# A four-layer graph network on one core: layer 3's graph loaded by transfers, a fourth attention tile, narrower projection matmuls, values spread through DRAM, and all jobs listed in a new order

## The chip, the core and the metric

The kernel runs on one core of a Trainium2 chip. Its engines are TensorE (PE, with its weight loads shown as PEld), VectorE (DVE), ScalarE (ACT), GpSimd (POOL) and SyncE (SP), which here only issues DMAs. Each engine works through its own list of instructions in order and waits on semaphores where it needs another's result. The metric is device time in microseconds, the median of several executions. All durations below are from one profiled execution.

## What is computed

There are 32 batches of 512 nodes with 64 features, and one 512 x 512 weighted graph `adj`, for the most part zero. Four layers follow one another; each normalises its input (layernorm, then maximum with 0), applies a graph network, and adds the result to its input:

```python
# layer 0: three steps, W1 and W2 are linear maps, v's node 0 is set to a given value
effects = adj @ v ; v = relu([v, effects] @ W1.T + b1) @ W2.T + b2
# layer 1: twice
z = relu((adj @ z) @ weights[i])
# layer 2: 8 heads with 64 -> 128 features, then one output attention of 64 features
h = x @ W ; s = (h @ h.T) * graph ; s = where(s == 0, -1e16, s)
out = softmax(s) @ h + b                 # leaky_relu(0.01) behind the heads, and behind the output
# layer 3: the graph's diagonal is set to 1
h = x @ w3 ; e = adj * leaky_relu(h @ a_src + (h @ a_dst).T, 0.2)
out = softmax(e) @ h + bias
```

## The kernel before

**Tiles.** Two batches make a pair; there are 16 pairs. Feature-by-node tiles hold two batches of 64 features on 128 partitions and 512 nodes in the free dimension. An attention tile `sm` is 128 x 8 x 512 (512 x 512 weights of one head, for two batches or two heads at a time by column groups); there are three such buffers, in the pool `ap`. PSUM is split into four buffers `s` for scores (`ps_s`) and four `mm` for all else (`ps_m`). A weighted sum takes all four `mm` buffers from its first part to its eviction.

**Stages of a pair.** `front` computes layers 0 and 1 in 25 steps F0 to F24: transposes (L327), per-node products (`by_nodes`, L347), aggregation over nodes (`aggregated`, L335, and L381), layernorms. Then come:

- eight units `Heads`, four for each batch of the pair: scores (`gram`, L445, with the mask added as a matmul at L448), row maxima with the graph as factor (L466, on DVE), their negation (L473, POOL), exponentials with row sums (L477, ACT), normalisation (reciprocal L487 on DVE, products L489 on POOL), transposition in blocks of 32 (L495, DVE). Units are taken two by two for the weighted sum (`weigh`, L505), its eviction `us` (L560), the head's matrix (L539), leaky ReLU into `y` (L550), and the projection (L568), whose result is collected in `cat` (L581, L584). The keys `Y` come from `ZZ` and the heads' Gram matrices (L827, L837).
- one unit `Out`: layer 2's output attention over `HH`. `features` (L589, L591) makes HH from cat by a matmul with II, which sums the two halves of the partitions and leaves the sum in both; `nodes` (L612, L598) transposes HH to node rows `hn`.
- the chain oA to oN: layernorm of x3, transposition to zT3, `weights` (L670, L672) for h3T, `nodes` (L681) for the rows h3n and the source terms `src` (L690, moved by four small DMAs, L695).
- one unit `Last`: layer 3. Its target row times ones (`pd`, L720) stays in one of the four `s` buffers; ACT's Prelu writes scores into sm (L722), and maxima are taken from there with the graph `A3` as factor, a second copy of adj in SBUF with ones on its diagonal (`loops`).

`Ends` (L779) sums the values of `Out` of one pair and `Last` of the pair before it together; its eviction is L798 and L800, its residuals L808 and L814. Inputs for keys are transposed twice for each pair (`features_of`, L419, once for each batch, z being laid out in two copies, L295). Values for the weighted sums must lie in groups of 32 partitions, four times over: `quarters` makes them by 16 DMAs of 32 KB each from tile to tile (L310), but for the last pair or two by a write to DRAM and four loads of 128 KB (L320, L304).

**Order.** Nothing is scheduled by the compiler: the order in which Python issues is the order on each engine. Each job (one score group, one maximum, one part of a sum) has a name and a place: `PLACES` gives a tick offset and a rank inside the tick, ten ticks make a round, and one round works on one pair's heads, on Out of the pair before, on Last of the pair before that, and on later pairs' fronts. `TAIL` lists the jobs behind the last regular tick; a short table places the jobs of the start. SP's DMAs are part of the jobs, so they stand in the same order, and a DMA that waits holds those behind it.

Of the kernel before, what the change touches and what calls it, by code (L numbers as in the profile page):

```python
# [21 lines left out]
def gnn_stack_kernel(  # L22
# [19 lines left out]

# [11 lines left out]

    def blk(t):
        return slice(t * P, (t + 1) * P)
# [7 lines left out]
    ap_ = ctx.enter_context(tc.tile_pool(name="ap", bufs=3))  # L80
# [6 lines left out]
    def mm_ps():  # L87

        return ps_m.tile([P, N], F32, tag="mm", name="mm")


# [12 lines left out]
    A3 = const.tile([P, NS, N], F32, name="A3")  # L104
    A2 = const.tile([P, NS, N], F32, name="A2")
    ident = const.tile([P, P], F32, name="ident")
# [3 lines left out]
    early1 = hp.tile([P, 4, P], F32, tag="h3T", bufs=1, name="early1")  # L110
# [3 lines left out]
    w3a = const.tile([P, P + 2], F32, name="w3a")  # L114
    w3bd = w3a[:, 0:P]
    a1bd = const.tile([P, 2], F32, name="a1bd")
    a2bd = const.tile([P, 2], F32, name="a2bd")
# [11 lines left out]
    for z0, value in ((mhalf, -0.5), (ones, 1.0), (NP, 0.0), (w3a, 0.0), (a1bd, 0.0), (a2bd, 0.0)):  # L129
        nc.gpsimd.memset(z0, value)  # L130
# [22 lines left out]
    for j, r in enumerate(R):  # L153
        nc.sync.dma_start(out=w3bd[r, r], in_=w3)
        nc.sync.dma_start(out=a1bd[r, j : j + 1], in_=a3[0:D, :])
        nc.sync.dma_start(out=a2bd[r, j : j + 1], in_=a3[D : 2 * D, :])
# [3 lines left out]


# [9 lines left out]
    II = const.tile([P, 2, D], F32, name="II")  # L171
    II2 = II.rearrange("p k d -> p (k d)")
    NEGM = const.tile([P, NT, N], BF16, name="NEGM")
    a2rep = const.tile([P, P], F32, name="a2rep")
# [11 lines left out]
    def graph_turned():  # L186
        for s in range(NT):
            pt = mm_ps()
            for t in range(NT):
                nc.tensor.transpose(pt[:, blk(t)], A[:, t, blk(s)], ident)  # L190
            (nc.scalar.copy, nc.vector.tensor_copy)[s % 2](AT[:, s, :], pt)
# [20 lines left out]
    def masks():  # L212

        for k in range(2):
            nc.vector.tensor_tensor(II[:, k, :], ident[:, 0:D], ident[:, D:P], ALU.add)

        nc.vector.tensor_scalar(NEGM, A, 0.0, NEG_INF, ALU.is_equal, ALU.mult)

    def loops():

        for s in range(NS):
            for base in (0, -D):
                nc.gpsimd.affine_select(
                    out=A3[:, s, hblk(s)],
                    in_=A3[:, s, hblk(s)],
                    pattern=[[-1, D]],
                    compare_op=ALU.not_equal,
                    fill=1.0,
                    base=base,
                    channel_multiplier=1,  # L230
                )
# [4 lines left out]

    def grams():

# [11 lines left out]
    def vectors():  # L250
        for j in range(2):
            nc.vector.tensor_scalar(a2rep[:, R[j]], ones[:, R[j]], a2bd[:, j : j + 1], None, ALU.mult)

        pt = mm_ps()
        nc.tensor.transpose(pt[:, 0:P], w3bd, ident)
        w3T = hp.tile([P, P], F32, tag="us", bufs=1, name="w3T")
        nc.vector.tensor_copy(w3T, pt[:, 0:P])
        pt = mm_ps()
        nc.tensor.matmul(pt[:, 0:2], lhsT=w3T, rhs=a1bd, start=True, stop=True)
        nc.vector.tensor_copy(w3a[:, P:], pt[:, 0:2])  # L260


    def ln_relu(xt, tag, bufs=2, copies=1):


# [18 lines left out]
        z = lp.tile([P, NT, 2, copies, D], F32, tag=tag, bufs=bufs, name="z")  # L284
        zf = z.rearrange("p t j c d -> p (t j) c d")
        nc.vector.scalar_tensor_tensor(  # L286
            zf[:, :, 0, :],
# [6 lines left out]
        if copies > 1:  # L294
            nc.gpsimd.tensor_copy(zf[:, :, 1, :], zf[:, :, 0, :])  # L295
        return z if copies > 1 else z[:, :, :, 0, :]

    def quarters(v, tag, rows=None):


        vq = hp.tile([P, N // 32, D], F32, tag=tag, bufs=1, name="vq")
        if rows is not None:
            for i in range(4):
                nc.sync.dma_start(  # L304
                    out=vq[32 * i : 32 * i + 32], in_=rows.rearrange("(jb r) d -> r jb d", r=32)
                )
            return vq
        for i in range(4):
            for k in range(4):
                nc.sync.dma_start(  # L310
                    out=vq[32 * i : 32 * i + 32].rearrange("r (t k) d -> r t k d", k=4)[:, :, k, :],
                    in_=v[32 * k : 32 * k + 32],
                )
        return vq

    def rows_of(v):

        rows = dr.tile([N, *v.shape[2:]], F32, tag=f"rows{len(v.shape)}", name="rows")
# [4 lines left out]
    def transposed(z, tag, bufs=2):  # L323

        pt = mm_ps()
        for t in range(NT):
            nc.tensor.transpose(pt[:, blk(t)], z[:, t].rearrange("p j d -> p (j d)"), ident)  # L327
        zT = lp.tile([P, N], F32, tag=tag, bufs=bufs, name="zT")
        nc.scalar.copy(zT, pt)
        return zT  # L330

    def aggregated(v, pe, first=True):

# [10 lines left out]

# [5 lines left out]
    def front(p, state):  # L350

# [10 lines left out]
        hT = transposed(v, "hT0")  # L362
        yield
        for step in range(STEPS):

# [16 lines left out]
            aggregated(v, ph, first=False)  # L382
            hT = lp.tile([P, N], F32, tag="hT0", name="hT0")
            nc.scalar.activation(hT, ph, AF.Relu, bias=b1k[k])
            yield
        pv = by_nodes(hT, W2T)
        x1 = xp.tile([P, NT, 2, D], F32, tag="x1", bufs=1, name="x1")
# [6 lines left out]
        for i in range(LAYERS):  # L394
            pe = mm_ps()
            aggregated(z, pe)
# [680 lines left out]
```

## Time and profile before

Three executions took 2306.47, 2307.35 and 2311.79 us; the median is 2307.35.

| | us | share of the span |
|---|---|---|
| profiled execution's own time, by its span | 2307.4 | |
| PE busy (matmuls) | 2186.1 | 95% |
| PEld busy (weight loads) | 1170.5 | 51% |
| DVE busy | 1858.7 | 81% |
| ACT busy | 1494.0 | 65% |
| POOL busy | 1299.3 | 56% |
| chain that ended last: PE / ACT / DVE / POOL | | 77% / 9% / 7% / 4% |
| DMA: 279,975 packets, 70.98 MB | | q1 (SP's): 17.1% of 16 engines |

A group's row reads: source line, engine, operation, output and input tiles, tile of the array, shape, count, then busy time, mean nanoseconds of one record, and the engine's idle time before the group with what ended it. An fp32 matmul shows as two records, so counts of such rows are twice those in the program. Rows in order of time begin with start and duration in microseconds. A row of a stretch has its bounds, its length, the busy times of PE, PEld, DVE, ACT and POOL with counts, the granted TensorE clock, and DMA.

The page's largest rows beside those shown in the prediction: exponentials (L477) 910.9 us on ACT, normalisation (L489) 871.3 on POOL, block transposes (L495) 769.8 and maxima (L466) 734.4 on DVE, scores (L445) 576.7 and weighted sums (L505) 500.9 on PE.

### The profile page before, as it was taken

To read this page: it belongs to the slowest core of one execution; us is meant where nothing else is said; L and a number is where in the kernel's file an instruction comes from. 1 tells how busy PE (TensorE), PEld (TensorE's weight loads), DVE (VectorE), ACT (ScalarE), POOL (GpSimd) and SP (SyncE) were. 2 spreads that over 40 slices of the span, in tenths; PEclk is the share of its full clock that TensorE was granted. 3 is DMA by queue.
4 is the path that set the end of the run, shared out by engine and by line. 5 is a ranking of instruction groups with operands and counts; after the bars stand their busy time and mean duration, and the time that the engine had idled before them with its cause. 6 is when DMAs were issued, how large, how long until landed. Compare 5 with 4: busy or idle time off the path is not lost.

```text
span 2307.4 us, 78438 instructions
## 1 busy us (share of the span) xinstructions
PE 2186.1 (95%) x32683; PEld 1170.5 (51%) x32683; DVE 1858.7 (81%) x4099; ACT 1494.0 (65%) x3754; POOL 1299.3 (56%) x2175
## 2 busy tenths in 40 slices
PE   7889999999999999999999999999999999998885
PEld 4335555555555555555554555555455555554443
DVE  3658788889888888988888898888889888888674
ACT  1446557667676666767666676766667676666564
POOL 2345465656656565665656566565656666565344
PEclk9899999999999999999999999999999999999987
DMA  5001111202121121212112121211212121021113
GB/s 123 11 15 21 25 21 23 42 15 39 20 41 27 21 42 17 38 21 39 29 19 42 19 39 20 36 32 18 41 21 36 23 31 32 15 37 23 29 29 57
DMA packets 279975, 70.98 MB, mean 31 GB/s; under 512 B 275004, under 2 KB 277060, under 8 KB 279620
## 3 DMA queue, kind: packets, MB, share of 16 engines
q1 hardware_dynamic: 278848, 65.80, 17.1%
q8 instruction: 256, 4.19, 0.8%
q14 instruction: 99, 0.81, 0.1%
q10 hardware_dynamic: 772, 0.17, 0.0%
HBM read 13.64 MB, written 4.98 MB: 8 GB/s over the span
## 4 chain that ended last, share of the span: by engine, by line
PE 77%; ACT 9%; DVE 7%; POOL 4%; issue 2%; DMA 1%; SPq 0%; ACTq 0%; POOLq 0%; DVEq 0%
PE s L445 21%; PE mm L505 16%; PE mm L335 10%; ACT sm L477 6%; PE mm L568 5%; PE mm L779 5%; PE mm L539 5%; PE s L448 5%; DVE sm L495 4%; PE mm L347 3%; PE mm L827 3%; DVE sm L466 2%; PE mm L381 2%; PE mm L612 1%; PE mm L589 1%
## 5 line engine op out<-in xcount | busy, mean ns | idle before, releaser
L477 ACT ACTIVATE sm<-sm,nmx 128x512 f32<-128x512 f32 x1280 | 910.9, 720 | 235.8 <-POOL nmx L473 235.4
L489 POOL TENSOR_SCALAR sm<-sm,rs 128x512 f32<-128x512 f32 x1280 | 871.3, 699 | 144.2 <-DVE rs L487 104.3
L466 DVE CUSTOM_DVE_ANT_0 sm<-s,A 128x512 f32<-128x512 f32 x1152 | 734.4, 679 | 138.3 <-PE s L448 113.5
L495 DVE STREAM_TRANSPOSE sm<-sm 128x1024 f32<-128x1024 f32 x640 | 769.8, 1224 | 38.6 <-POOL sm L489 37.7
L445 PE MATMUL s<-ZZ,Y 64*64 64x512 f32 x4096 | 576.7, 607 | 28.1 <-ACT Y L837 14.7
L505 PE MATMUL mm<-sm,vq 32*64 32x256 f32 (+1 forms) x17152 | 500.9, 378 | 24.5 <-DVE sm L495 11.4
L473 POOL TENSOR_SCALAR nmx<-mx 128x2 f32<-128x2 f32 x640 | 147.6, 234 | 582.1 <-DVE mx L466 526.8
L505 PEld LDWEIGHTS mm<-sm,vq 32*64 32x64 f32 x17152 | 399.2, 134 | 141.6 <-issue 62.1
L445 PEld LDWEIGHTS s<-ZZ,Y 64*64 64x64 f32 x4096 | 147.8, 133 | 256.8 <-issue 111.2
L448 PE MATMUL s<-NEGM,I2b 64*64 64x512 bf16 x2304 | 259.5, 378 | 0.0
L477 ACT ACTIVATION_READ_ACCUMULATOR sm<-sm,nmx 128x1 f32 x1280 | 250.7, 196 | 0.0
L560 ACT COPY us<-mm 128x256 f32<-128x256 f32 x256 | 76.2, 382 | 155.3 <-PE mm L505 155.0
L335 PE MATMUL mm<-AT,v 128*128 128x512 f32 x384 | 173.8, 595 | 0.0
L550 ACT ACTIVATE y<-mm,cols 128x512 f32<-128x512 f32 x256 | 159.2, 684 | 11.4 <-PE mm L539 11.3
L448 PEld LDWEIGHTS <-I2b 64*64 64x64 bf16 x2304 | 81.5, 107 | 160.5 <-issue 160.0
L273 POOL TENSOR_TENSOR xc<-x,nmu 128x512 f32<-128x512 f32 x48 | 54.8, 1141 | 182.9 <-DVE nmu L271 182.9
L539 PE MATMUL mm<-us,Wh 64*64 64x512 f32 x1024 | 134.0, 592 | 23.1 <-ACT us L560 23.1
L282 POOL TENSOR_TENSOR r<-ve,mhalf 128x8 f32<-128x8 f32 x64 | 110.8, 1731 | 45.2 <-DVE ve L280 41.4
L568 PE MATMUL mm<-y,Wo_sb 128*64 128x512 f32 x512 | 127.1, 605 | 0.0
L779 PE MATMUL mm<-sm,vq 32*64 32x256 f32 x3712 | 118.7, 381 | 4.0 <-DVE sm L495 2.6
L335 PEld LDWEIGHTS mm<-AT,v 128*128 128x128 f32 x384 | 73.5, 192 | 93.3 <-issue 92.5
L286 DVE SCALAR_TENSOR_TENSOR z<-xc,r 128x512 f32<-128x512 f32 x64 | 45.4, 709 | 93.2 <-POOL r L282 90.0
(135 smaller groups left out, 2073.6 us busy)
## 6 DMA issues: line engine op xcount, KB each, us to landing
vq<-z SPq DMA_DIRECT2D x512, 32.0 KB, 1.9
vq<-hn SPq DMA_DIRECT2D x480, 32.0 KB, 1.9
vq<-h3n SPq DMA_DIRECT2D x448, 32.0 KB, 1.9
A<-in_adj_dram SPq DMA_DIRECT2D x5, 1024.0 KB, 7.4
xt<-in_x_dram SPq DMA_DIRECT2D x32, 128.0 KB, 2.4
out_dram<-xo SPq DMA_DIRECT2D x32, 128.0 KB, 2.0
vq<-rows SPq DMA_DIRECT2D x24, 128.0 KB, 3.1
src<-src SPq DMA_DIRECT2D x64, 1.0 KB, 1.9
```

The lines of the kernel that those rows point to most:

```text
L335: nc.tensor.matmul(pe, lhsT=v[:, m].rearrange("p j d -> p (j d)"), rhs=AT[:, m, :], start=(first and m == 0), stop=(m == NT - 1),)
L445: nc.tensor.matmul(pss[half][R[ab], :], lhsT=lhsT, rhs=rhs, start=True, stop=False)
L448: nc.tensor.matmul(pss[half][R[ab], :], lhsT=I2b[R[half], :], rhs=NEGM[R[half], k, :], start=False, stop=True,)
L466: nc.vector.tensor_tensor_reduce(self.sm[:, s, :], src, graph, 1.0, -FMAX, ALU.mult, ALU.max, self.mx[:, s : s + 1])
L477: nc.scalar.activation(self.sm[:, s, :], self.sm[:, s, :], AF.Exp, bias=self.nmx[:, s : s + 1], accum_out=self.ssum[:, s : s + 1],)
L489: nc.gpsimd.tensor_scalar(self.sm[:, s, :], self.sm[:, s, :], self.rs[:, s : s + 1], 1.0, ALU.mult, ALU.mult)
L495: nc.vector.transpose(out=two, in_=two)
L505: nc.tensor.matmul(self.u[i][R[c], 0 : weights.shape[1] * 32], lhsT=values[32 * i : 32 * i + 32, jb, :], rhs=weights[32 * i : 32 * i + 32, ...
L539: nc.tensor.matmul(py[c][r, :], lhsT=Wh2[R[c], 2 * (self.q - 1 + c) + ab, r], rhs=self.us[R[c], 2 * ab : 2 * ab + 2].rearrange("p i (s e) ...
L550: nc.scalar.activation(y, py[c], AF.Prelu, bias=cols[:, h : h + 1], alpha=0.01)
L568: nc.tensor.matmul(pa[R[ab], :], lhsT=Wo_sb[:, h, :], rhs=self.y[h], start=(k == 0), stop=(k == 1),)
L779: nc.tensor.matmul(self.u[i][r, 0 : N // 2], lhsT=values[i // 2][q, jb, :], rhs=sm[q, :, 32 * jb : 32 * jb + 32], start=(jb == 0), stop=(j ...
```

## The change

- **Layer 3's graph.** A3 is no longer in SBUF. It is written once to DRAM (a copy of adj, with ones set on its diagonal by two DMAs), and for each pair `graphs` loads it in four slices of 512 KB into that pair's own attention tile (jobs g0e to g3e). `scores` of Last writes each block of 512 columns into an `s` buffer of PSUM, and the maxima read score and graph from there and from the tile.
- **Fourth attention tile.** The pool `ap` has four buffers.
- **Layer 3's target row.** w3a has two more columns, so that `nodes` yields source and target terms in one product. `values` (job oV) sends the target column to DRAM (`dst`), and `targets` (job de) loads it back into `pd`, spread over 64 partitions for each batch. The product h3T and the pd matmul are gone; the last pair makes pd by one matmul with w3d.
- **Projection by node halves.** `project` issues eight matmuls of 256 columns in place of four of 512. Partition half 0 of `cat` holds nodes 0 to 255, half 1 the others. HH is made from cat by four DMAs (job f), and hn by two transposes in place of four (jobs h and H).
- **Inputs transposed once.** z is no longer doubled. One set of four transposes gives ZZ for both batches; a second tile with the halves exchanged is filled by two DMAs (jobs zT and zE).
- **Values by way of DRAM**, in all pairs: rows are written once (`rows_of`), and four loads of 128 KB make each set of quarters.
- **Order.** Jobs are cut finer (evictions apart from the matmuls, negations apart from maxima; front has 33 steps), and three lists, HEAD, ROUND and TAIL, give all of them in one sequence. In ROUND a name carries the number of pairs by which it lags the round.

```diff
-    ap_ = ctx.enter_context(tc.tile_pool(name="ap", bufs=3))
+    ap_ = ctx.enter_context(tc.tile_pool(name="ap", bufs=4))
...
-    A3 = const.tile([P, NS, N], F32, name="A3")
+    A3 = dr.tile([P, NS, N], F32, tag="A3", bufs=1, name="A3")
...
-            nc.gpsimd.tensor_copy(zf[:, :, 1, :], zf[:, :, 0, :])
...
+    def quarters(rows, tag):
+        vq = hp.tile([P, N // 32, D], F32, tag=tag, bufs=1, name="vq")
+        for i in range(4):
+            nc.sync.dma_start(out=vq[32 * i : 32 * i + 32], in_=rows.rearrange("(jb r) d -> r jb d", r=32))
+        return vq
...
+    def features_of(p):
+        s = state[p]
+        pt = transposed(s["z"])
+        yield
+        s["ZZ"] = [lp.tile([P, N], F32, tag=f"ZZ{n}", name="ZZ") for n in range(2)]
+        nc.scalar.copy(s["ZZ"][0], pt)
+        for j in range(2):
+            nc.sync.dma_start(out=s["ZZ"][1][R[1 - j]], in_=s["ZZ"][0][R[j]])
+        yield
...
-                for k in range(2):
-                    for ab in range(2):
-                        h = 2 * (self.q - 1 + k) + ab
-                        nc.tensor.matmul(
-                            pa[R[ab], :],
-                            lhsT=Wo_sb[:, h, :],
-                            rhs=self.y[h],
+            order = [(k, ab) for ab in range(2) for k in range(2)]
+            for n, (k, ab) in enumerate(order):
+                for half in range(2):
+                    nc.tensor.matmul(
+                        self.pa[R[half], 0 : N // 2],
+                        lhsT=Wo_sb[:, self.head(k, ab), :],
+                        rhs=self.y[self.head(k, ab)][:, half * N // 2 : (half + 1) * N // 2],
...
-                nc.tensor.matmul(ph, lhsT=II2, rhs=self.cat, start=True, stop=True)
-                HH = hp.tile([P, N], F32, tag=f"HH{self.j}", bufs=1, name="HH")
-                nc.scalar.copy(HH, ph)
+            s["HH"][self.j] = hp.tile([P, N], F32, tag=f"HH{self.j}", bufs=1, name="HH")
+            for half in range(2):
+                for r in R:
+                    nc.sync.dma_start(
+                        out=s["HH"][self.j][r, half * N // 2 : (half + 1) * N // 2], in_=s["cat", self.j][R[half], :]
+                    )
...
-                nc.tensor.matmul(ph, lhsT=w3bd, rhs=s["zT3"], start=True, stop=True)
-                s["h3T"] = hp.tile([P, N], F32, tag="h3T", bufs=1, name="h3T")
-                nc.scalar.copy(s["h3T"], ph)
...
+            if self.p < NPAIR - 1:
+                s["dst"] = dr.tile([2, N], F32, tag="dst", name="dst")
+                for j in range(2):
+                    nc.sync.dma_start(out=s["dst"][j].rearrange("(t q) -> q t", q=P), in_=src[:, :, 2 + j])
+            self.rows3 = rows_of(h3n, "h3rows")
...
+        def graphs(self, k):
+            two = slice(2 * k, 2 * k + 2)
+            nc.sync.dma_start(out=self.sm[:, two, :], in_=A3[:, two, :])
+        def targets(self):
+            s = state[self.p]
+            if self.p == NPAIR - 1:
+                self.pd = score_ps()
+                nc.tensor.matmul(self.pd, lhsT=w3d, rhs=s["zT3"], start=True, stop=True)
+            else:
+                self.pd = hp.tile([P, N], F32, tag="pd", bufs=1, name="pd")
+                for j, r in enumerate(R):
+                    nc.sync.dma_start(out=self.pd[r], in_=s["dst"][j].partition_broadcast(D))
+        def scores(self, i):
+            self.pss[i] = score_ps()
+            nc.scalar.activation(
+                self.pss[i], self.pd, AF.Prelu, bias=state[self.p]["src"][:, i : i + 1], alpha=0.2
+            )
```

Two stretches of the new ROUND that the prediction speaks of, as they stand:

```
vD0:0 s0d:0 r7c:0 g2e:2 m2c:0 s1d:0 m3c:0 x2c:0 nAc:0 x3c:0 oN:2 nBc:0 s3d:0 us0:0 t1c:0 s2d:0 w00:0
oV:2 de:2 r2d:0 m1d:0 t3c:0 r7d:0 r6d:0 x1d:0 y00:0 m3d:0 s1f:1 nAd:0 r4d:0 r5d:0 k2:0
F15:-1 y10:0 o0:0 x3d:0 t0c:0 m2d:0 r3f:1 x2d:0 r2f:1 s3e:2
```

(s: a score group; r: a maximum; m: a negation; x: two exponentials; n: normalisation of half a tile; t: a block transpose; v: a quarter of a weighted sum; w, y, o, c: head matrix, leaky ReLU, projection, collecting; k, Y: keys. The last letter names the unit: a to d and g to j heads, f Out, e Last.)

## The prediction

> **What bounds the kernel now.** I read the page's table of busy times first, then the row of granted clock, then stretches of the span, then TensorE's instructions in order of time, then who waited for whom.
>
> ```profile
> span 2307.4 us, 78438 instructions
> PE 2186.1 (95%) x32683; PEld 1170.5 (51%) x32683; DVE 1858.7 (81%) x4099; ACT 1494.0 (65%) x3754; POOL 1299.3 (56%) x2175
> PEclk9899999999999999999999999999999999999987
> ```
>
> TensorE is busy 95% of the span, at full clock but for the two ends. Here a rule of the Trainium skill speaks against the plain reading: "Perfetto Trace Analysis", section "Identifying the Most-Contended Engine", holds that matmul busy time is no good measure of how near TensorE is to its limit, and wants the share of weight loads instead, which is only 51%. So I check by starts. One round of the loop (one pair of batches) in the steady middle:
>
> ```profile
> 1159.68 1.04 PE L539 MATMUL mm<-us,Wh 64*64 64x512 f32 x8
> 1160.54 1.04 PE L445 MATMUL s<-ZZ,Y 64*64 64x512 f32 x8
> 1161.40 0.40 PE L448 MATMUL s<-NEGM,I2b 64*64 64x512 bf16 x4
> 1161.61 1.04 PE L539 MATMUL mm<-us,Wh 64*64 64x512 f32 x8
> 1162.47 1.04 PE L827 MATMUL mm<-ZZ,G 64*64 64x256 f32 x16
> 1163.34 1.04 PE L445 MATMUL s<-ZZ,Y 64*64 64x512 f32 x8
> ```
>
> Start to start, a 512-column group takes 0.86 us although its record says 1.04: records overlap. L827, with half the columns and twice the instructions, takes 0.87: time follows columns streamed. The same L779 sum starts at 1094.88 and 1230.15, so a round is 135.3 us. Adding starts over that round (36 score groups at 1.07, five weighted sums at 7.1, five aggregations at 3.5, the rest about 37) gives 128.6 us of streaming. So TensorE really is the bound. Costs below are start to start. By the rule there would be half the engine to spare and nothing removed from TensorE would show; by the rows nearly all of it does.
>
> ```profile
> 203.10:1827.60 1624.50, 1595.28 (x24068) 853.03 (x24065) 1376.60 (x3038) 1106.59 (x2784) 960.62 (x1596) 1.00 0.17 29
> 2222.00:2307.40 85.40, 50.68 (x1138) 35.33 (x1136) 49.16 (x102) 43.50 (x109) 37.64 (x55) 0.79 0.34 57
> ```
>
> These are length, then busy time of PE, weight loads, DVE, ACT, POOL, then clock. In twelve rounds PE stands 29.2 us (2.4 a round); DVE is next at 85%. In the last 85 us nothing bounds but a chain of dependent steps, at clock 0.79.
>
> **What leaves TensorE.** The rows by form, and the same groups in order of time:
>
> ```profile
> L568 PE MATMUL mm<-y,Wo_sb 128*64 128x512 f32 x512 | 127.1, 605 | 0.0
> L589 PE MATMUL mm<-cat,II 128*128 128x512 f32 x64 | 33.0, 597 | 1.2 <-DVE cat L584 1.1
> L419 PE MATMUL mm<-ident,z 128*128 128x128 f32 x128 | 21.0, 287 | 1.8 <-POOL z L295 1.8
> L612 PE MATMUL mm<-ident,HH 128*128 128x128 f32 x128 | 20.0, 280 | 0.2 <-ACT HH L591 0.2
> L670 PE MATMUL mm<-zT,w3a 128*128 128x512 f32 x32 | 19.0, 676 | 2.0 <-ACT zT L329 2.0
> L720 PE MATMUL pd<-h3T,a2rep 128*128 128x512 f32 x32 | 17.2, 621 | 0.0
> ```
>
> ```profile
> 1193.34 1.13 PE L670 MATMUL mm<-zT,w3a 128*128 128x512 f32 x2
> 1194.31 1.06 PE L681 MATMUL mm<-w3a,zT 128*128 128x130 f32 x8
> ```
>
> Per round, from start to next start: L589 twice (0.96 and 0.86) is gone, cat now reaching HH by four transfers: 1.82. L670, whose product served only L720, goes: 0.97. L720 goes in 15 of 16 pairs, its row coming back by DRAM: 0.94. L419 is done once in place of twice: 0.49. The transposes of HH (0.59 and 0.53) are halved, cat holding two node halves on its partitions: 0.56. Sum 4.78 us; times 16, less one L720: 75.6 us. The busy column would say 33.0+10.5+10.0+19.0+16.1 = 88.6; I take the starts.
>
> **What is added there.** L681 grows from 130 to 132 columns: 0.01 us. Projection (L568) becomes eight matmuls of 256 columns for four of 512: the same columns, twice the weight loads, 64 times in all. Lower bound: 0, as L827 shows loads hidden at 256 columns. Upper bound: the eight extra record pairs' loads, 136 ns each but two at a time, 8 x 0.136/2 = 0.54 us, 35 us in all. A rule speaks against this edit: "TensorE: Matmul & The Clock Gate", section "Part 3: Packing small matmuls", says that a weight load overlaps a running matmul only where the row group differs, and these use all rows. At its loading figure (columns / 1.2 ns, same page, "LDWEIGHTS") 16 records would expose eight more loads of 53 ns: 0.43 us, an estimate of 27 us in all. But L335, all rows too, starts eight records in 3.43 us, 0.43 each, with 190 ns loads between them: they are hidden. I take 0.1 us a projection, 6.4 us; by the rule the sum would end near 2251.
>
> **What moves on the other engines**, hidden as long as PE sets the pace. DVE: cat copies and adds halve (675 to about 418 ns, the 128x256 rows of L814), 4 x 0.26; layer 3's maxima read PSUM as the others do (857 to 679), 8 x 0.18: 2.5 us a round less, 85% of a shorter round still. ACT: two copies of HH (585), one ZZ (584), one h3T (577): 2.3 less; layer 3's Prelu writes PSUM, bounded by 0.58 (copies) and 0.72 (exponentials), 0.69 taken. POOL: the copy of z, 0.6. Uncovered, DVE's saving would count only if DVE were the bound.
>
> **Transfers.** Before, SP issued 104 DMAs a round, 96 of them 32 KB pieces at 0.6 us each issue, about 60 us. After: 24 quarters (L304: 0.49), 8 for HH, 4 graph slices, 4+2 small columns, 2 for pd, 2 for ZZ, 4 row writes, 4 for x and out: 54, about 28 us. The graph's slices are 512 KB; 1 MB landed in 7.2 us, so about 3.6 to 7.2 each, loaded from late in one round to early in the next, into a tile that nothing else wants: off the path. Values go tile to DRAM to tile: write about 0.4 to issue and 2.4 to land (SP stood 2.4 at longest for it), then 4 x 0.49 and 3.1: about 7.9 us instead of 16 x 0.6 + 1.9 = 11.5. A waiting SP instruction now holds all behind it: the row write holds its quarters, and de (pd's load) holds the values q0, q1 and what follows. The lists put some TensorE work between each of these and its reader. Tightest is the second ZZ, whose two transfers stand between zE and k0: copy 0.58, two issues 1.2, landing 1.9, 3.7 us, against two w (0.92 each) and two score groups (1.07 each), 4.0 us. So I cost them at nothing; uncovered, one spreading costs up to 7.9 us a pair, one ZZ 3.7.
>
> **Fourth tile and order.** Waits for the last regular round (2041 to 2222 us):
>
> ```profile
> DVE sm L466 <- PE mm L505: 21.0, 3, 12.3
> PE s L445 <- DVE mx L466: 4.4, 3, 2.0
> PE mm L505 <- DVE sm L495: 4.4, 3, 2.8
> ```
>
> DVE waited 21 us for an attention tile to be released by a sum, and PE then waited for DVE: 4.4+4.4, with cat's 1.7 and 1.1, 11.6 us. Layer 3 holds its tile nearly a whole round now, so for the others three remain, nine units instead of ten. I take half: -6 us, bounds 0 and -11.6. At the start PE's 1.8 us wait for POOL's copy (L295) goes: -2. The last chain loses L670, its copy and Prelu-to-SBUF maxima (about 1+0.6+8 x 0.18 = 3) and gains issue and landing for HH (4 x 0.6+1.9, less 1.5 for L589 and its copy: 2.8): nothing. The new order otherwise is bounded from both sides by the rounds' own gap: it can close 2.4 us a round or open as much; I take 0, since both orders keep DVE and PE within some microseconds of work of each other.
>
> **Sum.** The profiled execution's span is 2307.4, the median of the runs 2307.35: nothing lies around it. 2307.4 - 75.6 + 6.4 - 6 - 2 = 2230.2. Forecast **2230 us**.
>
> **Rivals.** (A) The new order also closes the repeated gaps (each round PE waits 1.7 us for us, L560, and 0.7 for Y, L837). Evictions are jobs of their own now, which speaks for it; against, oN stands before us0 in the list and needs PSUM that us0 frees. 16 x 2.4 = 39 us more: 2191. (B) DVE, 85% busy and in order, becomes late more often, and PE's gap doubles: 8 score tiles of layer 3 pass through the four PSUM buffers that TensorE's scores need, where before one stayed. +39: 2269. (C) Slower: the small-column chain of layer 3. After oV, SP issues 4 src, 2 dst and one row write (7 x 0.65), dst must land (about 1.9) before de may issue two pd loads (1.2) that land 1.9 later: 9.6 us. Behind it ACT's first Prelu waits, and behind that ACT's exponentials and the evictions that free PSUM for TensorE. Before the Prelu the list gives ACT three pairs of exponentials (1.8 each) and two of Prelu (1.4), 8.2 us, so the shortfall is 1.4, and ACT idles 32%. For: SP and ACT are strict queues, and the 4-byte pieces of dst have no row of their own. Against: src, 256 such pieces, landed in 1.9. It decides from 4.8 us a round on TensorE ((75.6-6.4+8)/16); at three quarters of the chain, 7.2 us, it gives 2230 + 15 x 7.2 = 2338. (D) The removed matmuls were cover for waits, so that gaps grow by what is removed: about 2300; PE's few gaps speak against it.
>
> **How the numbers follow.** Forecast 0.58, A 0.18, B 0.11, C 0.10, D 0.03. What a measurement can tell from no change is 0.3%, 7 us. Faster: forecast, A, B, 0.87, with 0.01 of D; same: the other 0.02 of D; slower: C, 0.10. To leave out no more than 2 in 10, the range runs from just below A to just above B with the projection's upper bound: 2185 to 2290; C lies outside with 0.10, the tails of A and B with about 0.07. The forecast alone: 2212 to 2250.
>
> **What would show it.** A round (from one pair's last sum to the next) of 130.6 us in place of 135.3; no L589, L670 or L720 counterparts; the projection at 1.9 to 2.1 us start to start; PE's idle near 2.4 us a round; SP busy with under half the issues. Wrong if PE waits on layer 3's Prelu or on a DMA each round, if the projection takes over 2.5 us, or if the last chain is longer than 85 us.

## The result, and the profile after

The changed kernel takes 2365.1 us (median, 2360.2 to 2368.1) against 2307.8 for the kernel before, measured on the same chip: a ratio of 1.0242, 95% interval 1.0222 to 1.0262. It is slower by 2.4%, where 2230 us and a gain were forecast. The rival that came true is C, with a chance of 0.10 and a price of 2338 us.

First the page of the changed kernel: busy times, granted clock by slice, and the shares of the chain that ended last.

```profile
span 2366.4 us, 78289 instructions
PE 2146.3 (91%) x32943; PEld 1198.2 (51%) x32943; DVE 1823.3 (77%) x4098; ACT 1465.2 (62%) x3690; POOL 1256.7 (53%) x2142
PEclk9899999989999999999999999999999999999986
PE 74%; DMA 9%; ACT 5%; DVE 5%; issue 3%; SPq 2%; POOL 1%; ACTq 0%; DVEq 0%; POOLq 0%
```

TensorE has 40 us less to do (2186.1 before) and every other engine less too, but TensorE is busy 91% of the span in place of 95%. Transfers now make 9% of the chain that set the end (1% before). The work went down as planned, and waiting took more than its place.

Where does the time lie? The first full sum over both last layers is line 892 (779 before); thirteen of them stand in the listed rounds. The first and the last, TensorE in order of time:

```profile
410.97 7.16 PE L892 MATMUL mm<-sm,vq 32*64 32x256 f32 x256
...
2096.17 7.22 PE L892 MATMUL mm<-sm,vq 32*64 32x256 f32 x256
```

Twelve rounds take 1685.2 us, 140.43 each. Before, the same sum:

```profile
417.38 7.90 PE L779 MATMUL mm<-sm,vq 32*64 32x256 f32 x256
...
2041.87 7.90 PE L779 MATMUL mm<-sm,vq 32*64 32x256 f32 x256
```

That is 135.37 each. So the start is 6.4 us shorter, the rounds are 12 x 5.06 = 60.7 longer, and what follows is 270.2 in place of 265.5, 4.7 longer. The sum is +59.0, which is the difference of the two spans. The loss is in the rounds. Whom TensorE, ScalarE and SyncE's queue waited for over these twelve rounds (us in total, times, longest; one fence for each engine):

```profile
PE mm L452 <- ACT hT L491: 76.0, 11, 8.1
PE mm L619 <- issue: 15.5, 10, 2.4
```

```profile
ACT s L845 <- DMA vq<-rows: 39.6, 4, 10.4
ACT s L845 <- issue: 38.7, 4, 10.1
ACT s L845 <- DMA pd<-dst: 36.5, 4, 10.1
```

```profile
SPq L841 <- DMA dst<-src: 107.7, 14, 9.7
```

Read from the bottom: SyncE stands 7.7 us a time at line 841, the loads of pd, because dst has not landed. ScalarE stands about 9.6 us, once a round, at line 845, layer 3's first Prelu, which reads pd; the three rows give three names to one wait. TensorE stands 6.9 us, once a round, at line 452, since hT comes from ScalarE. The last step needs the order of time in one round:

```profile
1210.16 2.60 SPq L768 DMA_DIRECT2D src<-src  x4
1212.81 1.15 SPq L774 DMA_DIRECT2D dst<-src  x2
1214.06 0.45 SPq L417 DMA_DIRECT2D rows<-h3n  x1
...
1220.16 1.95 PE L680 MATMUL mm<-y,Wo_sb 128*64 128x256 f32 x16
1223.75 1.12 SPq L841 DMA_DIRECT2D pd<-dst  x2
...
1227.59 0.69 ACT L845 ACTIVATE s<-pd,src 128x512 f32<-128x512 f32 x1 [9.79 <-DMA vq<-rows]
1228.22 0.67 ACT L491 ACTIVATE hT<-mm,b1s 128x512 f32<-128x512 f32 x1
...
1228.94 2.07 PE L452 MATMUL mm<-W2T,hT 128*128 128x128 f32 x8 [6.83 <-ACT hT L491]
```

From the first issue of dst to the load of pd pass 10.9 us, and the Prelu starts 3.8 us after that. Behind the Prelu in ScalarE's queue stands hT for another pair of batches, and behind hT TensorE. The wait costs more than its length: in windows (us, then busy PE, weight loads, DVE, ACT, POOL, then clock, DMA share, GB/s)

```profile
1222.00:1226.00 4.00, 0.11 (x2) 0.00 (x0) 0.50 (x2) 0.00 (x0) 0.00 (x0) 1.00 0.23 51
1226.00:1230.00 4.00, 1.06 (x5) 1.06 (x6) 0.00 (x0) 2.41 (x5) 0.00 (x0) 0.53 0.82 151
1230.00:1234.00 4.00, 4.00 (x75) 2.62 (x79) 2.91 (x8) 3.28 (x6) 0.15 (x1) 0.62 0.25 58
```

TensorE comes back at a granted clock of 0.53 and 0.62 in these two windows: line 452 needs 2.0 us where such a group takes 1.1, and the 128 sum records after it 5.1 where they take 3.6. With the 6.8 of standing that is 9.2 us a round, and 140.4 less 9.2 would be 131.2: near the 130.6 that was forecast, with 1.3 us a round of gaps inside L619 (the second row of TensorE's waits above) still in it.

The other steps' rows: L589, L670 and L720 are gone. The projection of eight matmuls:

```profile
1253.19 1.95 PE L680 MATMUL mm<-y,Wo_sb 128*64 128x256 f32 x16
1255.06 1.16 PE L452 MATMUL mm<-NP,eT 128*128 128x128 f32 x8
```

It takes 1.87 us from start to start; before, 30.24 us for 16 of them (four rounds) make 1.89.

### The profile page after: what moved, and what is told of

The parts are those of the page before. It is cut to its first block, busy times and chain, and to the rows that moved or that the text cites. A ratio compares the mean times of both kernels' runs of the same rounds, so it can differ in the third digit from the quotient of the medians.

```text
span 2366.4 us, 78289 instructions
## 1 busy us (share of the span) xinstructions
PE 2146.3 (91%) x32943; PEld 1198.2 (51%) x32943; DVE 1823.3 (77%) x4098; ACT 1465.2 (62%) x3690; POOL 1256.7 (53%) x2142
## 4 chain that ended last, share of the span: by engine, by line
PE 74%; DMA 9%; ACT 5%; DVE 5%; issue 3%; SPq 2%; POOL 1%; ACTq 0%; DVEq 0%; POOLq 0%
PE mm L619 21%; PE s L563 18%; PE mm L441 10%; DMA dst<-src 6%; PE mm L452 5%; PE mm L892 5%; PE s L566 4%; PE mm L680 4%; PE mm L660 3%; DVE sm L572 2%; ACT sm L592 1%; DVE sm L610 1%; PE mm L487 1%; PE mm L939 1%; SPq L768 1%
## 5 line engine op out<-in xcount | busy, mean ns | idle before, releaser
L619 PE MATMUL mm<-sm,vq 32*64 32x256 f32 (+1 forms) x17152 | 526.7, 383 | 61.1 <-issue 35.1
L563 PE MATMUL s<-ZZ,Y 64*64 64x512 f32 x4096 | 566.4, 604 | 6.3 <-DVE mx L572 4.7
L619 PEld LDWEIGHTS mm<-sm,vq 32*64 32x64 f32 x17152 | 415.0, 137 | 179.2 <-issue 91.1
L585 POOL TENSOR_SCALAR nmx<-mx 128x2 f32<-128x2 f32 x640 | 136.4, 221 | 495.4 <-DVE mx L572 410.6
L566 PE MATMUL s<-NEGM,I2b 64*64 64x512 bf16 x2304 | 249.5, 378 | 0.0
L563 PEld LDWEIGHTS s<-ZZ,Y 64*64 64x64 f32 x4096 | 141.9, 132 | 202.1 <-issue 105.0
L845 ACT ACTIVATE s<-pd,src 128x512 f32<-128x512 f32 x120 | 78.0, 688 | 153.4 <-DMA pd<-dst 48.8
L566 PEld LDWEIGHTS <-I2b 64*64 64x64 bf16 x2304 | 79.6, 108 | 153.8 <-issue 149.7
L680 PE MATMUL mm<-y,Wo_sb 128*64 128x256 f32 x1024 | 128.7, 394 | 4.3 <-ACT y L672 4.3
L400 POOL TENSOR_TENSOR r<-ve,mhalf 128x8 f32<-128x8 f32 x64 | 105.8, 1654 | 43.6 <-DVE ve L398 42.1
L441 PE MATMUL mm<-AT,z 128*128 128x512 f32 x256 | 119.9, 612 | 5.8 <-DVE z L403 5.0
```

Of the source, the lines that this page charges most:

```text
L441: nc.tensor.matmul(pe, lhsT=v[:, m].rearrange("p j d -> p (j d)"), rhs=AT[:, m, :], start=(first and m == 0), stop=(m == NT - 1),)
L563: nc.tensor.matmul(pss[half][R[ab], :], lhsT=lhsT, rhs=rhs, start=True, stop=False)
L566: nc.tensor.matmul(pss[half][R[ab], :], lhsT=I2b[R[half], :], rhs=NEGM[R[half], k, :], start=False, stop=True)
L585: nc.gpsimd.tensor_scalar(self.small("nmx", two), self.small("mx", two), -1.0, None, ALU.mult)
L619: nc.tensor.matmul(self.u[i][R[c], 0 : weights.shape[1] * 32], lhsT=values[32 * i : 32 * i + 32, jb, :], rhs=weights[32 * i : 32 * i + 32, ...
L680: nc.tensor.matmul(self.pa[R[half], 0 : N // 2], lhsT=Wo_sb[:, self.head(k, ab), :], rhs=self.y[self.head(k, ab)][:, half * N // 2 : (half ...
```

## The experiments

The theories. 1: dst lands late, ScalarE's queue carries that to TensorE. 2: the new order costs, by PSUM buffers or VectorE, and the wait only covers it. Two more came with the first runs. 3: TensorE's instructions are fetched late when large transfers are under way. 4: the slow write holds the engines up by itself. A round below is the mean of twelve, from sum to sum as above.

**The row by matmul.** Target row by one matmul and a copy, no dst, no pd loads; `de` moved from behind oV to just ahead of k2, still ahead of its reader.

```diff
+            pd = score_ps()
+            nc.tensor.matmul(pd, lhsT=w3d, rhs=s["zT3"], start=True, stop=True)
...
                 self.pd = hp.tile([P, N], F32, tag="pd", bufs=1, name="pd")
-                for j, r in enumerate(R):
-                    nc.sync.dma_start(out=self.pd[r], in_=s["dst"][j].partition_broadcast(D))
+                nc.scalar.copy(self.pd, pd)
```

> The target row of layer 3 comes from one matmul (w3d by zT3) and an ACT copy again, made just ahead of k2; its two transfers to DRAM (dst) and two back (pd) are gone; all else is the changed kernel. Theory 1, the wait on dst: a round falls from 140.4 us by the 6.8 us that TensorE stands at the product behind ACT and by 2.4 us that its next groups lose at a lowered clock, and rises by one 512-column group, 0.94: 132.2 us; with the tail's two waits of 15 to 19 us cut to a few, 2366 - 11 x 8.2 - 20 = about 2255 us, no ACT wait on pd. Theory 2, the new order is what costs (score tiles of layer 3 pass through the four PSUM buffers, DVE late): the gap turns up at another wait, a round stays at 138 us or more, time 2340 to 2370.

Measured: 2266.5 us, ratio to before 0.9812 (0.9794 to 0.9830); a round 133.73. Theory 1 holds: undoing this one edit turns 2.4% slower into 1.9% faster, 98.6 us, with 1.06 us a round spent on the matmul. The granted clock is 0.99 to 1.00 in the rounds. The round is 1.5 us longer than expected; TensorE's longest wait in it had no partner, `PE mm L619 <- issue`, 16.0 us in nine rounds. It became theory 3.

**The Prelu later.** One job of the round's list moved.

```diff
-s3e:2 F16:-1 Y2:0 t0d:0 nBd:0 s1e:2
+F16:-1 Y2:0 t0d:0 nBd:0 s3e:2 s1e:2
```

> Transfers as in the changed kernel; in the twelve listed rounds one job, the first Prelu of layer 3 (s3e), stands behind F16, Y2, t0d and nBd in place of ahead of them, so ACT makes hT for TensorE's product before it waits for pd. Theory 1: dst still lands 10 to 11 us after its issue and ACT still waits, but TensorE has the product, 128 sum records and the next scores meanwhile: 5 to 9 us a round back, 2265 to 2310 us. Theory 2 (order or DVE sets the round): a round stays near 140 us, 2350 us or more.

Measured: 2357.8 us, ratio 1.0210 (1.0183 to 1.0236); a round 139.05. A miss: 1.4 us a round back, not 5 to 9. By its own forecast the run would speak for theory 2; the trace shows that it does not. The wait moved on. TensorE, ScalarE and VectorE in that version, in order of time:

```profile
1221.32 2.52 ACT L845 ACTIVATE s<-pd,src 128x512 f32<-128x512 f32 x4 [7.00 <-DMA pd<-dst]
...
1223.26 0.69 DVE L572 CUSTOM_DVE_ANT_0 sm<-s,sm 128x512 f32<-128x512 f32 x1 [6.94 <-ACT s L845]
...
1226.03 2.58 PE L563 MATMUL s<-HH 64*64 64x512 f32 x8 [5.96 <-DVE mx L572]
```

hT is made in time now, but VectorE's next maximum is layer 3's own, behind it stands the release of the score buffers, and TensorE's next scores want one. Three queues in fixed order all lead through pd; moving one reader changes only which of them brings the wait to TensorE.

**dst in 16-byte pieces.** The small columns lie with four nodes' values side by side, so that each dst transfer has 128 pieces of 16 bytes. The row comes back in order (q t), and Prelu reads it with a stride.

```diff
-            src = st.tile([P, NT, 4], F32, tag="src0", bufs=1, name="src")
+            src = st.tile([P, 4, NT], F32, tag="src0", bufs=1, name="src")
...
-                    nc.sync.dma_start(out=s["dst"][j].rearrange("(t q) -> q t", q=P), in_=src[:, :, 2 + j])
+                    nc.sync.dma_start(out=s["dst"][j].rearrange("(q t) -> q t", q=P), in_=src[:, 2 + j, :])
```

> Same transfers and same place, but dst is written as 128 pieces of 16 bytes a transfer (four nodes' values side by side) in place of 512 pieces of 4 bytes; Prelu reads the row with a stride of 16 bytes. If pieces set the landing: 10.7 us falls to about 3 to 4, ACT's wait of 10 us a round to 3 or less, TensorE's 6.8 goes: round about 131 us, time about 2245. If a write to DRAM costs 10 us whatever its pieces: landing, round and time as in the changed kernel, 2365.

Measured: 2281.0 us, ratio 0.9872 (0.9852 to 0.9893); a round 134.54. The pieces set the landing. The rest of the excess over 131 is the gap of theory 3 (16.9 us in ten rounds) and small waits for a ScalarE that has more to do: 1142 us in the twelve rounds in place of 1095, since a Prelu that reads with a stride takes 1.21 us for 0.69.

**dst into rows on chip.** The same 512 pieces of 4 bytes a transfer into two rows of a tile; two matmuls spread them over the partitions.

```diff
-                s["dst"] = dr.tile([2, N], F32, tag="dst", name="dst")
+                s["dst"] = hp.tile([P, N], F32, tag="pd", bufs=1, name="dst")[0:2]
                 for j in range(2):
-                    nc.sync.dma_start(out=s["dst"][j].rearrange("(t q) -> q t", q=P), in_=src[:, :, 2 + j])
+                    nc.sync.dma_start(out=s["dst"][j : j + 1], in_=src[:, :, 2 + j])
```

> dst goes as 512 pieces of 4 bytes a transfer into two rows on chip in place of DRAM; two 512-column matmuls and an ACT copy make pd from them, just ahead of k2. If it is DRAM as the target that makes small pieces slow: landing near the 1.9 us of src, round 131.2 + 2 x 0.9 = 133 us, 2275 us. If it is the number of 4-byte pieces: landing still near 10 us, now TensorE itself waits for it, and the time stays at 2350 or more.

Measured: 2331.4 us, ratio 1.0093 (1.0077 to 1.0109); a round 137.89, 3.8 us of it TensorE's wait for dst. The time lies between the two forecasts. The issue rows with KB each and median us to landing: first those of the changed kernel with only the graph slices moved (a run told below), whose profile has the median for the same three transfers,

```profile
pd<-dst SPq DMA_DIRECT2D x30, 128.0 KB, 3.0
src<-src SPq DMA_DIRECT2D x64, 1.0 KB, 1.9
dst<-src SPq DMA_DIRECT2D x30, 2.0 KB, 10.9
```

then dst with 16-byte pieces to DRAM,

```profile
dst<-src SPq DMA_DIRECT2D x30, 2.0 KB, 2.5
```

and dst with 4-byte pieces on chip.

```profile
dst<-src SPq DMA_DIRECT2D x30, 2.0 KB, 4.8
```

512 pieces of 4 bytes to DRAM land in 10.9 us, the same on chip in 4.8, the same 2 KB in 128 pieces to DRAM in 2.5. src, 256 pieces of 4 bytes on chip, takes 1.9. Here stands a rule of the Trainium skill that spoke against the row by DRAM and that the forecast did not weigh: "DMA: Bandwidth & Descriptors" says in its Specifications that a transfer under 512 bytes makes the DMA read, modify and write, and its section "Why small descriptors are slow (HBM only)" exempts transfers within the chip's own memory from what makes small pieces slow. By that rule src was the wrong row to price dst by. The trace agrees on the target (10.9 against 4.8). But the same pieces are not free on chip either: 4.8 against 1.9 for half as many, where dst goes to one partition a transfer and src to 64, and no run keeps number and spread apart. And 16 bytes, far below 512, were enough here.

**The graph slices early.** On the version by matmul, g2e moved; it is one slice, a transfer of 512 KB.

```diff
-r7c:0 g2e:2 m2c:0
+r7c:0 m2c:0
...
-F12:-1 ZQ0:0 r1c:0
+F12:-1 ZQ0:0 g2e:2 r1c:0
```

What led to it: of the nine gaps in the version by matmul three starts of TensorE, and SyncE's queue around the last of them.

```profile
893.25 4.08 PE L619 MATMUL mm<-sm,vq 32*64 32x256 f32 x80 [2.45 <-issue]
1028.95 2.41 PE L619 MATMUL mm<-sm,vq 32*64 32x256 f32 x77 [1.60 <-issue]
1162.77 2.40 PE L619 MATMUL mm<-sm,vq 32*64 32x256 f32 x75 [1.40 <-issue]
```

```profile
1155.83 0.38 SPq L417 DMA_DIRECT2D rows<-hn  x1
1156.26 0.50 SPq L823 DMA_DIRECT2D sm<-A  x1
1156.86 2.39 SPq L704 DMA_DIRECT2D HH<-cat  x4
1159.35 3.59 SPq L424 DMA_DIRECT2D vq<-rows  x4
```

The gap lies inside one sum, where nothing is waited for, and moves by two or three instructions a round (80, 77, 75 are left after it): a place counted in instructions, not in data. Three kinds of transfers had queued behind H1's row write, and all four, 1.4 MB, start just ahead of it. The trace can say which instructions. Two stretches from one resumption to the next, with the counts of matmuls and weight loads, and the queue that brings in blocks of instructions (packets, MB, share of 16 engines):

```profile
621.78:756.13 134.35, 131.59 (x2036) 72.63 (x2035) 112.87 (x256) 91.73 (x231) 78.40 (x134) 1.00 0.26 57
756.13:893.25 137.12, 133.80 (x2035) 73.25 (x2036) 113.38 (x256) 91.73 (x231) 78.92 (x135) 0.99 0.26 57
```

```profile
q8 instruction: 259, 4.24, 0.8%
```

With TensorE's waiting instructions counted too, each of the nine resumptions lies 4096 records behind the one before. The queue brought 259 blocks of 16 KB for TensorE's 66,382 records, 256 to a block: the place is the edge of a block, every sixteenth. The gaps of the changed kernel (ten) and of the version with 16-byte pieces (ten) lie at the same count.

> On the version with the target row by matmul: in the listed rounds the third and fourth graph slices (g2e, 512 KB) are issued after ZQ0, about 35 us earlier, when no transfer is under way, in place of right behind H1's row write. That version stands 1.4 to 2.5 us in each round in the middle of a weighted sum, at a fixed count of TensorE instructions and waiting for nothing shown, while row write, graph slices, HH and quarters (1.4 MB) are all in flight. Theory 3, the fetch of TensorE's instructions waits behind these transfers: the gap falls to 1 us or less, 2266 - 12 x 1.2 = about 2252 us. If the gap has to do with the values of the sum or with the program alone: gap and time unchanged, 2266.

Measured: 2240.9 us, ratio 0.9709 (0.9695 to 0.9723); a round 131.74. The gaps are gone, and 25.6 us, 24 of them in the rounds: 16.0 of gaps, and 7.9 that TensorE is busy less, for which no run gives a reason. Theory 3's forecast was 14. The edge of the block is passed at the same count as before, now without a stop, and the records of the queue say what changed. Ahead of the nine gaps the block begins to load 2.8 to 3.9 us after TensorE entered the block before, and TensorE resumes 1.3 to 1.5 us after it has landed; with the slice moved it begins after 0.5 to 1.3 us. So theory 3 is shown in this: TensorE stands at the edge of a block that comes late, and it comes late because of when the slice is sent. Not shown is what in the transfers holds its start back.

**HH early too.** On top of that, f1 right behind c3.

```diff
-w00:0 f1:1 t2c:0
+w00:0 t2c:0
...
-t1b:0 c3:1 m1c:0
+t1b:0 c3:1 f1:1 m1c:0
```

> As graph_early, and the four transfers of HH (f1, 512 KB written) right after cat (c3), ahead of H1's row write, so that only row write and quarters are left at the place of the gap. Theory 3: gap gone, 2266 - 12 x 1.6 = about 2247 us. Else as graph_early.

Measured: 2242.4 us, ratio 0.9708 (0.9692 to 0.9724); a round 131.82. Nothing more to gain. (The four transfers of HH are 64 KB each, 256 KB.)

**The graph slices alone.** The same g2e move on the changed kernel.

> The changed kernel with the third and fourth graph slices issued after ZQ0 and nothing else. The gap in the sum (0.8 to 2.4 us a round) goes, but the row's transfers start by the same work and are waited for as before: if the gap lies ahead of oV, all of it shows, 2365 - 11 x 1.5 = 2349; if the wait on dst takes it up, 2362 or more.

Measured: 2356.2 us, ratio 1.0216 (1.0197 to 1.0234); a round 139.28, 1.15 less. The gaps in the sum are gone here too. Alone the move is worth 9 us by the medians, with intervals that overlap, between the two forecasts; TensorE's wait for hT takes up a part (79.5 us in the twelve rounds for 76.0).

**Layer 3's chain early.** The changed kernel, transfers as they are; in the rounds oN, oV and de stand ahead of the sum vA0, with h1 and H1 before them.

```diff
-t2b:0 oT:2 h1:1
-s2c:0 s3c:0 m0c:0 r4c:0 x1c:0 vA0:0 oE:2 x0c:0 r6c:0 vB0:0 H1:1 r5c:0 vC0:0
+t2b:0 h1:1 oT:2
+H1:1 oE:2 s2c:0 s3c:0 oN:2 m0c:0 r4c:0 oV:2 de:2 x1c:0 vA0:0 x0c:0 r6c:0 vB0:0 r5c:0 vC0:0
```

> The changed kernel with every transfer as it is (512 pieces of 4 bytes to DRAM, two reads back), but in the listed rounds layer 3's nodes, values and target row (oN, oV, de) and h1, H1 ahead of them stand before the sum vA0 in place of after us0 and w10: some 14 us earlier against the first Prelu; the last rounds as they are. Theory 1, dst is slow and its wait costs because the lead is short: ACT's wait on pd is gone in the rounds, round 140.4 to about 131.5 to 133, time 2265 to 2285 us. If the transfers cost through contention or SP's queue wherever they stand: 2340 or more.

Measured: 2344.2 us, ratio 1.0157 (1.0142 to 1.0172); a round 138.04. A miss by 60 us. ScalarE's wait on pd is gone, as expected, and time was lost elsewhere: while dst landed, all four engines stood for 2 to 7 us. That was theory 4.

**Both early.** ov_early with g2e and f1 moved as above.

> Both moves on the changed kernel: oN, oV, de early, and graph slices and HH early. If both theories hold the gains add: 2250 to 2262 us, a round near 130.6 as forecast for the changed kernel; if the gap in the sum was only where another wait would have been, as ov_early.

Measured: 2326.1 us, ratio 1.0071 (1.0056 to 1.0086); a round 137.3. A miss for the same reason.

**A write that nobody reads.** The version by matmul with graph slices early (2240.9) gets the two dst writes back at their old place.

```diff
+            if self.p < NPAIR - 1:
+                s["dst"] = dr.tile([2, N], F32, tag="dst", name="dst")
+                for j in range(2):
+                    nc.sync.dma_start(out=s["dst"][j].rearrange("(t q) -> q t", q=P), in_=src[:, :, 2 + j])
             self.rows3 = rows_of(h3n, "h3rows")
```

> The version with the target row by matmul and the graph slices early (2241 us), with the two dst writes of 512 4-byte pieces put back at their place; nothing reads them, so no instruction can wait for their data. In the run with oN, oV and de early, TensorE, VectorE and ScalarE each stood 4 to 7 us in the round while dst was landing, waiting for nothing of it. Theory 4, the write itself holds up the engines: 3 to 7 us a round more, 2280 to 2330 us, and idle time without a waited-for partner until the write lands. If dst costs only through the wait on its data: 2241 to 2245.

Measured: 2255.5 us, ratio 0.9764 (0.9745 to 0.9783); a round 131.79 against 131.74. The writes land in 11.1 us (median) and cost nothing in the rounds; what they cost lies behind them (265.5 us against 253.1), where TensorE waits 6.0 us more for VectorE's transposes and 3.2 more for nothing that the profile names. So neither forecast is met: at this place in the rounds theory 4 falls, and the last pairs are not explained.

**16-byte pieces with the two moves.** dst in 16-byte pieces with g2e early; with oN, oV, de early; with both.

> dst as 128 pieces of 16 bytes (2281 us) with the graph slices early. Theory 3: the gap of 1.4 us in the sum goes as it did with the matmul version (2266 to 2241): 2281 - 12 x 1.6 = about 2260.

> oN, oV and de early (2344 us) with dst as 128 pieces of 16 bytes. Theory 4: with short landing the engines' standstill of 4 to 7 us a round goes: round 138.0 to about 133, 2344 - 12 x 5 = about 2284 or less. If the early place itself is what costs (PSUM buffers, h3n shared with H1): 2330 or more.

> All three: oN, oV, de early, dst in 16-byte pieces, graph slices early. If the three causes are separate and all there is, a round near the 130.6 us forecast for the changed kernel: 2240 to 2262.

Measured: 2256.9 us (ratio 0.9774, 0.9755 to 0.9793; a round 132.42), 2254.1 (0.9757, 0.9742 to 0.9772; 132.30) and 2246.6 (0.9726, 0.9709 to 0.9742; 131.93). At the early place the short landing is worth 90 us, more than the 84 at the late place where something waited for it. So the early place alone was not at fault; it took the 512 pieces as well. The third still makes the row by transfers, as the change meant to.

**The unread write at the early place.** oN and oV early, the row by matmul ahead of k2: once without dst, once with the unread writes as above.

> oN, oV early as in ov_early, but the target row by matmul ahead of k2 and no dst transfers: the control for ov_unread. No wait on dst and no standstill: about as the matmul version, with the gap in the sum possibly elsewhere: 2245 to 2270.

> As ov_pd with the two dst writes of 512 4-byte pieces issued at the early place and read by nothing. If the write itself holds up the engines at this place: 4 to 7 us a round over ov_pd, that is 50 to 85 us. If the standstill in ov_early came from SP waiting on dst with everything else queued behind it: within 15 us of ov_pd, as at the old place.

Measured: 2239.7 us (ratio 0.9709, 0.9694 to 0.9723; a round 131.60) without, 2330.0 (1.0096, 1.0077 to 1.0114; 137.86) with. 6.3 us a round and 90 in all for a write whose data no instruction wants: theory 4 holds here. In one round with it, SyncE's issues and two windows of all engines:

```profile
1189.94 1.16 SPq L774 DMA_DIRECT2D dst<-src  x2
...
1192.24 7.34 SPq L704 DMA_DIRECT2D HH<-cat  x4
```

```profile
1192.00:1196.00 4.00, 3.79 (x75) 1.74 (x59) 2.49 (x2) 1.20 (x4) 2.70 (x4) 1.00 1.39 58
1196.00:1200.00 4.00, 0.00 (x0) 0.00 (x0) 0.26 (x1) 0.00 (x0) 0.00 (x0) 1.00 1.02 37
```

Four microseconds in which nothing computes, while the transfers are busy at 37 GB/s; and the four issues of HH take 7.3 us in place of 2.4. Who waits for whom in this stretch, and VectorE's row for the twelve rounds:

```profile
1194.32 0.40 PE L566 MATMUL s<-NEGM,I2b 64*64 64x512 bf16 x4
...
1199.74 0.69 DVE L572 CUSTOM_DVE_ANT_0 sm<-s,A 128x512 f32<-128x512 f32 x1 [5.07 <-remote]
...
1200.50 2.58 PE L563 MATMUL s<-ZZ,Y 64*64 64x512 f32 x8 [4.71 <-DVE mx L572]
...
1201.39 0.72 ACT L592 ACTIVATE sm<-sm,nmx 128x512 f32<-128x512 f32 x1 [5.61 <-POOL nmx L585]
```

```profile
DVE sm L572 <- remote: 38.8, 10, 6.5
```

It is one wait with three behind it. TensorE's scores are on record as done at 1194.7; VectorE's maximum of them starts 5 us later, released by nothing that the profile can name ("remote"); TensorE, GpSimd and ScalarE wait for that maximum. The trace also records when semaphores are raised. The one that the maximum waits for, which the L566 matmuls raise, goes up at 1199.72, and between 1194.75 and 1199.63 no semaphore goes up at all, neither an engine's nor a transfer's. A silence of 2.5 to 4.9 us stands in each of the ten rounds with the write at the early place; without dst, with 16-byte pieces there, or with the unread write at the late place, none in the rounds is over 1.4. So the signals of finished work come late (or the matmuls themselves, as the profile models their ends).

Late blocks of instructions are a rival cause, since a block in flight with dst is slow: 3.5 us in this round, where those of the version without dst take 0.9 to 1.6. But these standstills lie at no fixed count of TensorE's instructions. And a slow block is neither needed nor enough. In a row for one microsecond the share times 16 us is the time that the packet took; the first is from 1326 us of this version, the second from the unread write at the late place, with the windows of all engines behind it:

```profile
q8 instruction: 1, 0.02, 5.8%
```

```profile
q8 instruction: 1, 0.02, 23.8%
```

```profile
1816.00:1820.00 4.00, 4.00 (x33) 1.99 (x26) 3.71 (x11) 4.00 (x12) 3.07 (x6) 1.00 0.92 57
1820.00:1824.00 4.00, 4.00 (x24) 1.65 (x22) 4.00 (x8) 3.33 (x9) 2.64 (x5) 1.00 1.32 18
```

The first block took 0.9 us, and TensorE stood 4.7 us from 1331.2; the second took 3.8, beside dst, and TensorE stayed busy. That the write holds up the engines at the early place is shown, and that what comes late is the signalling. Why the write does so there and not 15 us later stays open: in the run with graph slice and HH moved away (2326.1 us) VectorE's unnamed waits are still 32.7 us, so that burst is not the reason.

## Why the prediction was wrong

**The step that failed** is the sentence "So I cost them at nothing", and under it, in rival C, dst "must land (about 1.9)". Its row was src: 256 pieces of 4 bytes within the chip. dst has twice the pieces in each transfer, and they go to DRAM: 10.9 us. The chain from oV on, put at 9.6 us, is 17.4 in the trace (from 1210.16 to 1227.59), and ScalarE's work ahead of the Prelu covers 7.6 of it (it goes idle at 1217.8): 9.8 us uncovered where C's own sum had 1.4. The sign of being wrong that the prediction named, TensorE behind layer 3's Prelu each round, is the one that came. C's mechanism was right to the engine, Prelu holding ScalarE and ScalarE holding TensorE; C said itself that the 4-byte pieces of dst had no row of their own. Its size was off, 9.2 us a round for 7.2, and so was its chance of 0.10: a price with no row near it should have been bounded from above before it was called hidden.

**A term left out** is the lowered clock after standing: 2.4 of the 9.2 us.

**A cost not seen** is the gap in the sum: 15.5 us in the rounds of the changed kernel. Transfers were counted by SyncE's issue time and by their landing, but not for what they do to the blocks of TensorE's instructions.

**Removed from TensorE** (4.78 us a round): right. Starts over four rounds of the version with graph slices early: L589, L670 and L720 gone (1.82, 0.96, 0.94), transposes of z 1.61 for 2.01, of HH 0.68 for 1.12: 4.56. The rule that the prediction set against this, weight loads at 51%, comes from the Trainium skill's "Perfetto Trace Analysis", "Identifying the Most-Contended Engine", which asks for the share of peak arithmetic as well; the prediction left that out. By it nothing would have shown; the rounds came down from 135.37 to 131.60 us once the waits were gone.

**The projection** (+0.1 each, by the rule 0.43): nothing, 1.87 against 1.89. The Trainium skill's rule on weight loads that use all rows ("TensorE: Matmul & The Clock Gate", "Part 3: Packing small matmuls") did not show in this shape; the nearest row, L335, had said so.

**Fourth tile** (-6): VectorE's 21 us of waiting for a tile have no row in the profile after; what that was worth was not measured apart. **Head and tail**: the start is 6.4 us shorter and the end 4.7 longer, where -2 and 0 stood.

**The order** (0 either way): with both waits out of the way TensorE no longer waits for us or Y (1.7 and 0.7 a round before), the first part of rival A. But it takes back about 2 us: the five sums 37.6 for 36.9, the transposes of yT 1.5 for 0.9, the aggregations 17.9 for 17.5, the columns of line 749 1.1 for 0.9.

**What was left of the forecast**: 131.60 us a round with oN and oV early and the row by matmul. Less the matmul's 1.06 that is 130.5, where 130.6 was forecast. So close a match is partly luck, since the order gave 2.4 and took about 2 where the forecast had nothing. The arithmetic on TensorE held; the part that was not computed on TensorE decided.

## What to carry to other kernels

Price each transfer by its pieces and by where they go, and take a row with the same target: the two 2 KB rows of dst were among the smallest transfers by bytes and took 10.9 us to land. When a small value must cross the partitions, try a matmul (1.06 us here, and a copy on ScalarE) before a way through DRAM, and if it has to be DRAM lay the data out so that one piece carries several values. When a wait is found, shorten what is waited for: moving one reader moved the wait to another queue, and moving the slow write earlier made it stall engines that did not need it.

## What was not expected of the hardware

A write of two times 512 pieces of 4 bytes to DRAM, read by nothing, cost 6.3 us a round at one place of the program and 0.05 at another; at the first no semaphore went up for 2.5 to 4.9 us a round. Bursts of 1.4 MB of transfers opened gaps of 1.4 to 2.5 us in TensorE's stream at the edge of a block of 256 of its instructions; sending 0.5 MB of them some 34 us earlier closed them. Cutting 2 KB into 128 pieces for 512 shortened its landing from 10.9 to 2.5 us. TensorE stood for 6.8 us, and in the window of 4 us in which it resumed and in the next its granted clock was 0.53 and 0.62.
